# Deformable sampling by matrix multiplication: twelve column tiles of 11 in place of eleven of 12

## The chip, the cores and the metric

The kernel runs on one core of a Trainium2 chip. A core has TensorE (PE, the matrix engine; its weight loads are shown apart as PEld), VectorE (DVE), ScalarE (ACT), GpSimd (POOL) and SyncE (SP, which here only issues DMAs). The metric is the device time of one execution in microseconds (us); three runs of the kernel before give a median of 6642.1 us. "ns of one" is the mean duration of one instruction in one profiled execution.

## The reference

The input is x, 2 images of 256 channels and 128 x 128 pixels, float32. Two layers follow each other. In the first, a group-normalised x goes through three branches that differ in their dilation (1, 9, 12). Each branch predicts an offset for each of 9 taps and each pixel, samples the image bilinearly at the moved place, weights the nine samples per channel and adds them; a layer norm and a GELU follow. Their sum, a 1x1 convolution and a small MLP with two layer norms end the layer. The second layer is a 3x3 convolution with weights quantised to three values. Cut to the part that the change touches:

```python
off = _conv(x, w_off, pad, dil)                      # 18 planes: dy, dx of 9 taps
py = yy[None, None] - pad + ky * dil + off[:, :, 0]  # ky, kx: the tap
px = xx[None, None] - pad + kx * dil + off[:, :, 1]
sampled = _bilinear(x, py, px)                       # [B, C, 9, H, W]
y = jnp.einsum('bckhw,ck->bchw', sampled, w.reshape(C, 9))
```

## The kernel before

**Stages.** Stage A (to about 920 us) normalises x, writes it with the pixels as rows into a table in DRAM (`tables`, a row of 256 channels for every pixel of a padded image WT columns wide), predicts the offsets and writes "hats": for each tap, pixel and row or column of a window, the bilinear weight. Stage B (920 to 5700 us) samples and runs the MLP. Stage C (from 5700 us) is the second layer's convolution.

**Sampling.** A bilinear sample is a weighted sum over pixels near the unmoved place, so a tile of output columns is one matrix product. A window is RI = 2 rows of the padded image, which gives 66 windows per image, 132 in all. The 132 padded columns (W + 2 * REACH) are cut into NT = 11 tiles of CI = 12. A tile's sources are TR x TC = 6 x 16 = 96 pixels, two more on each side, so PX = 96 partitions. `load_tiles` (L1316) loads them from the table, 96 KB per tile, into buffers named xs; there are 18. For each window and branch (a "unit", 396 of them) `build` (L1353) multiplies row hats hy and column hats hx on DVE into A, 96 partitions x 9 taps x 2 rows x 156 columns (L1367). `sample` (L1442) then runs two passes, one per half of the channels. In a pass each tile is one product (L1468): the pixels of the tile are the stationary operand, the A of that tile's columns for all 9 taps and 2 rows are the moving one, 18 runs of 12 columns, 216 in all. In the profile a float32 product is two MATMUL instructions, each with its LDWEIGHTS. The result lands in PSUM, in one of four banks `pm` that hold two tiles each; ScalarE copies a bank to `ev` (L1480, or L1488 where taps are missing). A pass has six banks: tile 0 alone, then (1,2), (3,4) to (9,10). Then `accumulate` (L1375) adds the nine taps into a ring of image rows: one activation per new row on ScalarE (L1411), the others on VectorE (L1429). There are three `ev` buffers, two A, three hy and three hx.

`columns` (L1431) names which of the three column taps reach a tile at all. With dilation 12 the first and the last tile lack one column tap, so their product is 144 columns instead of 216. The columns of a tile which lie in the padding are computed all the same and not used.

**Order.** TensorE, VectorE and ScalarE run stage B in program order (`pin`). The MLP, layer norms and the rest of the first layer are written as generators, and `tail.advance()` runs a piece of them once at the beginning of a pass and once in its middle (L1458), so their matmuls (L890, L905, L1133, L1137, L1154) stand between the banks of the sampling. All loads of stage B are issued by SP, in an order that a scheduler lays down: per window 11 loads of xs and 18 of hats. A load of xs waits until the product that last read its buffer is done. With 18 buffers and 11 tiles in use, 7 tiles of the next window are loaded early, and its last four follow when tiles 0 to 3 of the present window have been read for the last time, in its sixth pass.

**Constants that hang on CI.** WT is the width of the table; XCLS lists the tap shifts modulo CI, for the patterns with which stage A forms the column hats; SPAN is how far from a tile's middle an offset may reach before a separate list of missed samples is used.

Of the kernel before, what the change touches and what calls it, by code (L numbers as in the profile page):

```python
# [9 lines left out]
F32 = mybir.dt.float32  # L10
# [10 lines left out]
W = 128  # L21
C = 256
# [6 lines left out]
DILS = (1, 9, 12)  # L29
# [8 lines left out]


REACH = 2  # L40
RI, CI = 2, 12
TR, TC = RI + 2 * REACH, CI + 2 * REACH
NT = -(-(W + 2 * REACH) // CI)
PX = TR * TC
WT = NT * CI + 2 * REACH
AO = 12
WA = 28 + W
NH = TR + TC + 2
# [5 lines left out]
PEAK = 4  # L54
GAP = 2
LAG = 7
XCLS = (0, 1, 3, 9, 11)
SLOTS = 42
ROWS = P
EACH = 2  # L60
SPAN = (REACH + (RI - 1) / 2, REACH + (CI - 1) / 2)
NPAT = RI + len(XCLS) + 1


# [7 lines left out]
def conv_preact_kernel(ctx: ExitStack, tc: tile.TileContext, t: dict, out: bass.AP):  # L72
    nc = tc.nc
    x = t["x"]
    NB, _, H, _ = x.shape
# [84 lines left out]

    tables = scratch.tile([NB * HT * WT, C], F32, name="tables")
    table = [tables[b * HT * WT : (b + 1) * HT * WT] for b in range(NB)]

# [46 lines left out]
    reach = const.tile([P, 2, NB * H], F32, name="reach")  # L210
# [110 lines left out]
    def phase_a(b, pool, psum, k, beside, todo):  # L321
        mean, rstd = gn1[b]
        tv = table[b].rearrange("(y x) c -> y x c", x=WT)
        zero = k["zero"]

        for y0, y1 in ((0, 2 * REACH), (2 * REACH + H, HT)):
            for yy in range(y0, y1):
                for x0 in range(0, WT, P):
                    n = min(P, WT - x0)
                    nc.sync.dma_start(tv[yy, x0 : x0 + n, :], zero[0:n])  # L330
        for x0, x1 in ((0, 2 * REACH), (2 * REACH + W, WT)):
            for xx in range(x0, x1):
# [170 lines left out]
    def missing(psum, pool, tabs):  # L503

        def tmp(name, rows, n, dt=F32):
            return pool.tile([rows, n], dt, name=name, tag=name, bufs=1)
# [11 lines left out]
        top = tmp("top", P, 8)  # L518
        nc.vector.tensor_scalar(V, reach[:, 0], SPAN[0], None, ALU.is_gt)
        nc.vector.scalar_tensor_tensor(V, reach[:, 1], SPAN[1], V, ALU.is_gt, ALU.max)  # L520
        nc.vector.tensor_reduce(cnt, V, AX.X, ALU.add)
# [84 lines left out]
        for d in range(2):  # L606
# [3 lines left out]
            for c in range(2):  # L610
                nc.vector.tensor_scalar(cd[:, c], cd[:, c], SPAN[c] ** 2, None, ALU.is_le)
            cov.append(cd)
# [95 lines left out]
    with ExitStack() as actx:  # L708
# [24 lines left out]
        for b in range(NB):  # L733
            stats = ap.tile([P, KC, NGRP, 6], F32, name=f"stats1_{b}", tag=f"stats1_{b}")
            for c in range(KC):
                for g0 in range(0, NGRP, XT):
                    xt = ap.tile([P, XT * NG], F32, name="xt", tag="xt", bufs=3)
# [527 lines left out]
    def sample_near(pool, psum, k):  # L1265

        pin = tc.keep_in_program_order
# [8 lines left out]
        xts, hbs, owners, begun = {}, {}, {}, set()  # L1276
# [38 lines left out]

        def load_tiles(b, Rt):  # L1316

            xts[b, Rt] = []
            for T in range(NT):
                xt = pool.tile([PX, C], F32, name="xs", tag="xs", bufs=18)  # L1320
                src = bass.AP(
                    table[b].tensor,
                    table[b].offset + (Rt * RI * WT + T * CI) * C,
                    [[C, TC], [WT * C, TR], [1, C]],
                )
                nc.sync.dma_start(xt, src)
                xts[b, Rt].append(xt)

        def taps(u):
            return [ky for ky in (-1, 0, 1) if valid(units[u][1], units[u][2], ky)]  # L1330
# [99 lines left out]

        def columns(br, T):  # L1431

            dil = DILS[br]
            kept = [
                i
                for i, s in enumerate((-dil, 0, dil))
                if max(0, REACH + s) < (T + 1) * CI
                and T * CI < min(W + 2 * REACH, W + REACH + s)
            ]
            return kept[0] * RI, (kept[-1] + 1) * RI  # L1440

        def sample(u, c):  # L1442

            b, Rt, br = units[u]
            kys = taps(u)
            tail.advance()
            if not kys:
                tail.advance()
                if c == KC - 1:
                    prepare(u + 2)  # L1450
                return
            A = k["A"][u % len(k["A"])].rearrange("p (y t) i w -> p y (t i) w", y=3)
            y0, y1 = kys[0] + 1, kys[-1] + 2
            n = (y1 - y0) * 3 * RI * CI
            ev = pool.tile([P, 9 * RI, NT * CI], F32, name="ev", tag="ev", bufs=3)
            evv = ev.rearrange("p (y m) w -> p y m w", y=3)
            for T in range(-1, NT, 2):
                if T == 2 * ((NT + 1) // 4) - 1:  # L1458
                    tail.advance()
                ts = range(max(T, 0), T + 2)  # L1460
                pm = k["pm"][tail.banks % len(k["pm"])]
                tail.banks += 1
                pv = pm[:, :, 0:n].rearrange("p j (y m w) -> p j y m w", y=y1 - y0, w=CI)
                reach = [columns(br, t) for t in ts]
                for j, t in enumerate(ts):
                    m0, m1 = reach[j]
                    pin(
                        nc.tensor.matmul(  # L1468
                            pv[:, j, :, m0:m1, :],
                            lhsT=xts[b, Rt][t][:, c * P : (c + 1) * P],  # L1470
                            rhs=A[:, y0:y1, m0:m1, AO + t * CI : AO + (t + 1) * CI],
                            start=True,
                            stop=True,
                        )
                    )
                m0, m1 = min(r[0] for r in reach), max(r[1] for r in reach)
                if m1 - m0 == 3 * RI:
                    dst = ev[:, y0 * 3 * RI : y1 * 3 * RI, ts[0] * CI : (ts[-1] + 1) * CI]
                    pin(
                        nc.scalar.copy(  # L1480
                            dst.rearrange("p m (t j) -> p t m j", j=CI),
                            pm[:, 0 : len(ts), 0:n].rearrange("p t (m j) -> p t m j", j=CI),
                        )
                    )
                else:
                    assert len(ts) == 1
                    pin(
                        nc.scalar.copy(  # L1488
                            evv[:, y0:y1, m0:m1, ts[0] * CI : (ts[0] + 1) * CI],
                            pv[:, 0, :, m0:m1, :],  # L1490
                        )
                    )
            if c == KC - 1:
                prepare(u + 2)
            accumulate(u, c, ev, kys)

        def prepare(u):

            if u < len(units):
                for ky in taps(u):  # L1500
                    build(u, ky)
                    load_hats(items.index((u, ky)) + 3)

        items = [(u, ky) for u in range(len(units)) for ky in taps(u)]
        load_hats(0)
        load_tiles(*units[0][0:2])
        load_hats(1)
        load_hats(2)
# [5 lines left out]
        for u, (b, Rt, br) in enumerate(units):  # L1514
            if u % len(BRS) == 0 and u + len(BRS) < len(units):
                load_tiles(*units[u + len(BRS)][0:2])
            for c in range(KC):
                sample(u, c)
            if u == 1:
                tail.extra = lacking(pool, tail.tile, miss, pin)  # L1520

            for b, br, g in begins[u]:
                r0 = g * R % RINGS[br]
                ring = k["rings"][br][:, :, r0 : r0 + R, :].rearrange("p k r w -> p k (r w)")
                tail.begin(tail.branch(b, br, g, ring), LAG)
                if br == 0:
                    begun_groups += 1
                    spot(begun_groups)
# [93 lines left out]
    with tc.If(beyond > 0) as cmp:  # L1622
        with ExitStack() as bctx:
            psum = bctx.enter_context(tc.tile_pool(name="ps_g", bufs=1, space=PSUM))
            pool = bctx.enter_context(tc.tile_pool(name="gpool", bufs=1))
            for b in range(NB):
                sample_any(b, pool, psum)
    with cmp.Else():
        with ExitStack() as bctx:
            psum = bctx.enter_context(tc.tile_pool(name="ps_b", bufs=1, space=PSUM))  # L1630
            pool = bctx.enter_context(tc.tile_pool(name="bpool", bufs=1))
# [359 lines left out]
```

## Time and profile before

| | |
|---|---|
| median of 3 runs | 6642.1 us (6639.65 to 6650.33) |
| profiled execution, its own time | 6632.7 us |
| its span on the core | 6630.8 us |
| stage B in it | 920 to 5700 us, 4780 us |
| mean granted TensorE clock | 0.974 |
| VectorE busy, share of the span | 89% |
| ScalarE busy, share of the span | 63% |
| loads of xs, whole run | 1452 of 96 KB |
| loads of hy and of hx, whole run | 1112 and 1112 in the page's row, of 288 KB |

A group's row names the line, the engine, the operation, what it writes and reads, the shape and the count; then the busy time and the mean duration of one; then the idle time of the engine just before such instructions and what ended it. A MATMUL's duration includes its latency: two that follow each other overlap in the record, and what one costs is the distance from its start to the next one's start. The chain of waits goes back from the last instruction through what released each, and gives each line's share of the time.

### The profile page before, as it was taken

How to read it: one execution, taken by the hardware profiler on the slowest of the kernel's cores; microseconds unless marked ns; L12 is line 12 of the kernel's file. 1: busy time of each engine (PE TensorE's matmuls, PEld its weight loads, DVE VectorE, ACT ScalarE, POOL GpSimd, SP SyncE). 2: the span in 40 equal slices, each digit the busy share in tenths (PEclk: the TensorE clock that was granted, in tenths of full speed). 3: DMA queues.
4: the chain of work that ended last, by engine and by line, in shares of the span. 5: the costliest groups of instructions: out<-in, count | busy, mean ns of one | idle time of the engine just before them, and what ended most of it. 6: DMA issues, size and time to landing. Idle time of an engine off the chain costs nothing.

```text
span 6630.8 us, 100591 instructions
## 1 busy us (share of the span) xinstructions
PE 6275.4 (95%) x32242; PEld 4993.0 (75%) x32242; DVE 5906.2 (89%) x13772; ACT 4189.3 (63%) x8690; POOL 686.7 (10%) x665
## 2 busy tenths in 40 slices
PE   6899978999999999999999999999999999989999
PEld 3455558888888888888888888888888888734444
DVE  8766668999999999999778999999999999689996
ACT  2344447777777777777676777777777777554442
POOL 0000000111111111111110111111111111200000
PEclk9999978999999999999999999999999999989999
DMA  8976667877787777787667877788777777343332
GB/s 290 274 214 199 201 169 216 226 217 219 223 225 217 223 217 224 222 222 206 181 194 203 227 219 219 221 223 227 223 217 220 215 222 209 122 164 132 139 139 90
DMA packets 635795, 1360.49 MB, mean 205 GB/s; under 512 B 109592, under 2 KB 290344, under 8 KB 618736
## 3 DMA queue, kind: packets, MB, share of 16 engines
q1 hardware_dynamic: 617328, 1318.97, 68.9%
q10 hardware_dynamic: 17408, 33.56, 1.6%
q8 instruction: 261, 4.28, 0.3%
q14 instruction: 286, 2.34, 0.1%
q0 software_dynamic: 512, 1.34, 0.1%
HBM read 1087.10 MB, written 266.47 MB: 204 GB/s over the span
## 4 chain that ended last, share of the span: by engine, by line
PE 53%; DVE 30%; DMA 8%; ACT 5%; issue 3%; SPq 0%; POOL 0%; DVEq 0%; ACTq 0%; POOLq 0%
PE pm L1468 22%; DVE ring L1429 13%; PE pc L1810 6%; PE hp L890 6%; PE h L1137 5%; DVE A L1367 5%; PE pz L364 4%; DMA hx<-hats 3%; PE pc L1137 3%; DMA xa<-in_x 3%; ACT ev L1480 2%; ACT v L1115 2%; DVE st L1101 1%; PE ph L463 1%; PE tp L905 1%
## 5 line engine op out<-in xcount | busy, mean ns | idle before, releaser
L1468 PE MATMUL pm<-A,xs 96*128 96x216 f32 (+2 forms) x17424 | 3248.5, 343 | 176.4 <-ACT ev L1480 45.4
L1468 PEld LDWEIGHTS pm<-A,xs 96*128 96x128 f32 x17424 | 3049.1, 195 | 374.1 <-ACT ev L1480 119.2
L1429 DVE SCALAR_TENSOR_TENSOR ring<-ev,defw,ring 128x256 f32<-128x256 f32 (+4 forms) x6372 | 2481.2, 451 | 98.1 <-ACT ev L1480 47.8
L1480 ACT COPY ev<-pm 128x432 f32<-128x432 f32 (+4 forms) x4488 | 1987.5, 483 | 869.3 <-PE pm L1468 695.8
L1367 DVE TENSOR_TENSOR A<-hy,hx 96x768 f32<-96x768 f32 (+1 forms) x1124 | 1009.5, 945 | 164.1 <-DMA hx<-hats 89.8
L1107 POOL TENSOR_TENSOR rs<-rs,mhalf 128x4 f32<-128x4 f32 x320 | 472.0, 1475 | 4202.5 <-DVE rs L1106 3543.9
L1810 PE MATMUL pc<-cring,signs 128*128 128x512 bf16 x3456 | 757.9, 382 | 17.0 <-ACT cring L1727 7.4
L1115 ACT ACTIVATE v<-v,rs 128x256 f32<-128x256 f32 x1280 | 694.4, 594 | 16.7 <-POOL rs L1108 16.6
L1810 PEld LDWEIGHTS <-signs 128*128 128x128 bf16 x3456 | 339.6, 98 | 434.6 <-issue 27.7
L890 PE MATMUL hp<-S,w 128*128 128x512 f32 x1024 | 493.9, 607 | 0.8 <-ACT S L1221 0.8
L364 PE MATMUL pz<-wz,xa 128*128 128x486 f32 x1024 | 461.6, 578 | 25.3 <-DVE zr L371 25.3
L1137 PE MATMUL h<-w,hT 128*128 128x256 f32 x2048 | 477.1, 379 | 0.0
L1101 DVE BATCH_NORM_STATS2 st<-v 128x6 f32<-128x256 f32 x1280 | 446.9, 410 | 30.8 <-ACT v L921 30.8
L1411 ACT ACTIVATE ring<-ev,defw 128x256 f32<-128x256 f32 (+1 forms) x856 | 404.5, 485 | 24.2
L1137 PEld LDWEIGHTS h<-w,hT 128*128 128x128 f32 x2048 | 369.3, 190 | 65.5 <-issue 1.0
L364 PEld LDWEIGHTS pz<-wz,xa 128*128 128x128 f32 x1024 | 189.2, 191 | 189.3 <-issue 126.1
L921 ACT COPY v<-tp 128x512 f32<-128x512 f32 x384 | 207.8, 598 | 182.7 <-PE tp L913 182.4
L1230 ACT ACTIVATE hT<-hp,b 128x512 f32<-128x512 f32 x256 | 176.1, 688 | 218.6 <-PE hp L890 214.6
L890 PEld LDWEIGHTS hp<-S,w 128*128 128x128 f32 x1024 | 196.7, 197 | 139.4 <-issue 121.3
L470 ACT ACTIVATE hb<-ph 96x512 f32<-96x512 f32 (+1 forms) x384 | 209.8, 596 | 144.2 <-PE ph L463 135.6
L1137 PE MATMUL pc<-convw,xn 128*128 128x256 f32 x1024 | 271.1, 393 | 2.4 <-ACT xn L1202 2.4
L371 ACT COPY zr<-pz 128x486 f32<-128x486 f32 x128 | 72.1, 564 | 256.5 <-PE pz L364 253.8
(246 smaller groups left out, 5132.5 us busy)
## 6 DMA issues: line engine op xcount, KB each, us to landing
hy<-hats SPq DMA_DIRECT2D x1112, 288.0 KB
hx<-hats SPq DMA_DIRECT2D x1112, 288.0 KB
xs<-tables SPq DMA_DIRECT2D x1452, 96.0 KB
g12d<-v SPq DMA_DIRECT2D x128, 512.0 KB
other<-g12d SPq DMA_DIRECT2D x128, 512.0 KB
hats<-hb SPq DMA_DIRECT2D x64, 720.0 KB
hats<-hb SPq DMA_DIRECT2D x64, 576.0 KB
xa<-in_x ACTq DMA_DIRECT2D x64, 512.0 KB
```

Source lines behind the costliest of these rows:

```text
L364: nc.tensor.matmul(pz[:, 0:NZ], lhsT=xt[:, c, r, :], rhs=k["wz"][:, c, :], start=c == 0, stop=c == KC - 1,)
L890: nc.tensor.matmul(out, lhsT=w, rhs=v, start=i == 0, stop=i == n - 1)
L1101: pin(nc.vector.bn_stats(st[:, j, :], rows[j]))
L1107: nc.gpsimd.tensor_tensor(rs[:, 0, :], rs[:, 0, :], mhalf[:, 0:n], ALU.pow)
L1115: nc.scalar.activation(row, row, func, scale=rs[:, 0, j : j + 1], bias=rs[:, 1, j : j + 1])
L1137: nc.tensor.matmul(bank[:, j, :], lhsT=v[:, px], rhs=w, start=False, stop=i == len(pairs) - 1,)
L1367: nc.vector.tensor_tensor(dst, hy[:, i0:i1].rearrange("p i t w -> p t i w"), hx[:, i0:i1].rearrange("p i t w -> p t i w"), ALU.mult,)
L1411: pin(nc.scalar.mul(dst, src, w))
L1429: pin(nc.vector.scalar_tensor_tensor(dst, src, w, dst, ALU.mult, ALU.add))
L1468: nc.tensor.matmul(pv[:, j, :, m0:m1, :], lhsT=xts[b, Rt][t][:, c * P : (c + 1) * P], rhs=A[:, y0:y1, m0:m1, AO + t * CI : AO + (t + 1) * CI],
L1480: nc.scalar.copy(dst.rearrange("p m (t j) -> p t m j", j=CI), pm[:, 0 : len(ts), 0:n].rearrange("p t (m j) -> p t m j", j=CI),)
L1810: nc.tensor.matmul(pc, lhsT=signs[:, k, (h * 3 + t) * 3 + kx, m * P : (m + 1) * P], rhs=xc[:, i, k, t * JC : (t + 1) * JC, kx : kx + W], s ...
```

## The change

The 132 padded columns are cut into 12 tiles of 11 columns. A tile's sources stay 6 x 16 pixels, so the loads still fill 96 partitions: 2 columns before the tile and 3 after it. WT goes from 136 to 137. The banks of a pass are (1,2), (3,4) to (9,10) and, last, the pair of the first and the last tile (0,11); these two are loaded last. `columns` now also gives the first and last column that any tap uses, and a product covers only those; its result lies densely in its half of the bank. All six copies take two tiles. The buffers xs go from 18 to 19. The piece of the tail in the middle of a pass comes after two banks (four tiles) in place of three banks (five tiles).

```diff
-RI, CI = 2, 12
-TR, TC = RI + 2 * REACH, CI + 2 * REACH
+RI, CI = 2, 11
+TR, TC = RI + 2 * REACH, 16
 NT = -(-(W + 2 * REACH) // CI)
-WT = NT * CI + 2 * REACH
+WT = (NT - 1) * CI + TC
+SIDE = (TC - 1) / 2
-XCLS = (0, 1, 3, 9, 11)
+XCLS = (0, 1, 2, 9, 10)
-SPAN = (REACH + (RI - 1) / 2, REACH + (CI - 1) / 2)
+SPAN = (REACH + (RI - 1) / 2, SIDE)
...
-            xts[b, Rt] = []
-            for T in range(NT):
-                xt = pool.tile([PX, C], F32, name="xs", tag="xs", bufs=18)
+            xts[b, Rt] = {}
+            for T in (*range(1, NT - 1), 0, NT - 1):
+                xt = pool.tile([PX, C], F32, name="xs", tag="xs", bufs=19)
...
-            dil = DILS[br]
-            kept = [
-                i
-                for i, s in enumerate((-dil, 0, dil))
-                if max(0, REACH + s) < (T + 1) * CI
-                and T * CI < min(W + 2 * REACH, W + REACH + s)
-            ]
-            return kept[0] * RI, (kept[-1] + 1) * RI
+            p0, p1 = T * CI, (T + 1) * CI
+            kept, lo, hi = [], p1, p0
+            for i, s in enumerate((-DILS[br], 0, DILS[br])):
+                a, z = max(p0, 0, REACH + s), min(p1, W + 2 * REACH, W + REACH + s)
+                if a < z:
+                    kept.append(i)
+                    lo, hi = min(lo, a), max(hi, z)
+            return kept[0] * RI, (kept[-1] + 1) * RI, lo, hi
...
-            for T in range(-1, NT, 2):
-                if T == 2 * ((NT + 1) // 4) - 1:
+            edges = (0, NT - 1)
+            for ts in [(t, t + 1) for t in range(1, NT - 1, 2)] + [edges]:
+                if ts[0] == NT // 2 - 1:
                     tail.advance()
...
-                    m0, m1 = reach[j]
+                    m0, m1, p0, p1 = reach[j]
+                    w, n = p1 - p0, (y1 - y0) * (m1 - m0) * (p1 - p0)
                     pin(
                         nc.tensor.matmul(
-                            pv[:, j, :, m0:m1, :],
+                            pm[:, j, 0:n].rearrange(
+                                "p (y m w) -> p y m w", y=y1 - y0, w=w
+                            ),
                             lhsT=xts[b, Rt][t][:, c * P : (c + 1) * P],
-                            rhs=A[:, y0:y1, m0:m1, AO + t * CI : AO + (t + 1) * CI],
+                            rhs=A[:, y0:y1, m0:m1, AO + p0 : AO + p1],
...
+                (ma, mb, pa, _), (md, _, pd, pe) = reach
+                first = evv[:, y0:y1, ma:mb, pa : pa + w]
+                step = (md - ma) * NT * CI + pd - pa
...
+                dst = bass.AP(
+                    first.tensor, first.offset, [dims[0], [step, 2]] + rows + [dims[3]]
+                )
...
+                pin(nc.scalar.copy(dst, src))
```

## The prediction

> **What bounds the kernel now.** I read the page's shares first, then the busy times of stage B alone, then the chain of waits of that stage, then the timeline of TensorE, for the price of one product. The page:
>
> ```profile
> span 6630.8 us, 100591 instructions
> PE 6275.4 (95%) x32242; PEld 4993.0 (75%) x32242; DVE 5906.2 (89%) x13772; ACT 4189.3 (63%) x8690; POOL 686.7 (10%) x665
> ```
>
> Stage B alone (columns: stretch, its length, then busy us and instructions of each engine, granted clock, DMA share, GB/s) and its chain of waits:
>
> ```profile
> 920.00:5700.00 4780.00, 4614.24 (x24864) 4115.21 (x24865) 4451.02 (x11227) 3415.48 (x7664) 653.15 (x618) 0.98 0.77 216
> ...
> by line: PE pm L1468 31.0%; DVE ring L1429 17.5%; PE hp L890 7.3%; PE h L1137 6.4%; DVE A L1367 6.3%; DMA hx<-hats 4.5%; PE pc L1137 3.4%; ACT ev L1480 3.3%; issue 3.2%; ACT v L1115 2.1%; DVE st L1101 1.9%; PE tp L905 1.8%; DMA xs<-tables 1
> ```
>
> TensorE is idle for 166 of 4780 us, VectorE for 329: both are nearly full, TensorE more so. The chain says the same: over half of it is TensorE, some 26% VectorE (ring, A, st). So a stretch of TensorE time saved is not a stretch of kernel time saved wherever VectorE leads.
>
> Now the price of a product, from TensorE's timeline (start, length of the merged group, what, count):
>
> ```profile
> 3028.74 2.35 PE L1468 MATMUL pm<-A,xs 96*128 96x216 f32 x12
> 3030.93 0.27 PE L1133 MATMUL h<-row,ones 128*128 128x256 bf16 x1
> 3031.05 1.89 PE L1137 MATMUL h<-w,hT 128*128 128x256 f32 x8
> 3032.77 0.27 PE L1133 MATMUL h<-row,ones 128*128 128x256 bf16 x1
> ```
>
> Twelve instructions of 216 columns take 3030.93 - 3028.74 = 2.19 us, 183 ns each; eight of 256 columns take 1.72 us, 215 ns each. Both are 0.845 ns per column: there is no fixed price per product at these sizes, although the first reads 18 runs of 12 columns and the second one run. In the records of the smaller forms of L1468 the starts are 123 ns apart for 144 columns (again 0.85 each) but 112 ns for 72: below about 131 columns a floor holds.
>
> The waits of the line, and the two kinds of copy (rows: group, count | busy, mean ns | idle before, releasers):
>
> ```profile
> L1468 PE MATMUL pm<-A,xs 96*128 96x216 f32 x14304 | 2846.4, 352 | 126.6 <-ACT S L1221 41.5 <-ACT ev L1480 27.8 <-ACT ev L1488 23.4
> L1480 ACT COPY ev<-pm 128x432 f32<-128x432 f32 x3440 | 1680.5, 524 | 523.1 <-PE pm L1468 490.3
> L1480 ACT COPY ev<-pm 128x216 f32<-128x216 f32 x480 | 156.2, 326 | 228.6 <-DVE ring L1429 122.7 <-PE pm L1468 101.9 <-PE tp L913 3.7
> L1488 ACT COPY ev<-pm 128x144 f32<-128x144 f32 x208 | 55.9, 269 | 87.5 <-DVE ring L1429 76.1 <-PE pm L1468 9.5 <-DVE st L1101 1.6
> ```
>
> ScalarE waits mostly for products; the first copy of a pass (216 or 144) waits for VectorE to free an `ev`. A copy costs about 0.9 ns per element: (524 - 326) / 216.
>
> **What the Trainium skill says.** "TensorE: Matmul & The Clock Gate", section Back-to-back issue gap, gives N / 2.4 + 2.5 ns for a warm stream, so a cost by columns; the trace agrees in kind, at two cycles per column for each of a float32 product's two instructions. The same page, section LDWEIGHTS, prices a weight load by its columns, P / 1.2, 107 ns for 128; the measured floor of 112 ns fits it. "Perfetto Trace Analysis", section Matmuls, says larger matmuls are more efficient; from 144 to 256 columns the trace shows no difference. "SBUF — State Buffer", section Door 1, says SBUF has 16-byte lines and that crossing into a new one costs; runs of 12 floats that begin on a line, as now, show no such price, and runs of 11 are not in this trace.
>
> **The change part by part.**
>
> *Products, removed and added.* With all three row taps, a pass costs before 11 x 216 = 2376 columns (dilations 1 and 9) or 9 x 216 + 2 x 144 = 2232 (12). After: ten tiles of 18 x 11 = 198, and two edge tiles: 18 x 10 = 180 each with dilation 1 (columns 1 to 10 and 121 to 130 of the padded image), 12 x 11 = 132 each with 9 and 12, as one column tap never reaches them. That is 2340, 2244 and 2244. So the cut into 11s as such costs nothing (12 x 198 = 11 x 216), and what is saved is the padding and, with dilation 9, a tap at each edge. Over all windows, those with fewer row taps included, the compiled instruction list of the kernel before has 7152 products of 216, 1200 of 144 and 360 smaller; that of the kernel after 6880 of 198, 512 of 180, 1664 of 132 and 448 of at most 88. At 0.845 ns per column, not less than 111, two instructions each: 2983 us before, 2929 after, so **-54 us of TensorE**. The 792 more products are in this, and their loads of weights lie behind the matmuls as now.
>
> *How much reaches the end.* The chain holds line 1468 for 0.31 x 4780 = 1482 us, half of its 2983; at that share -27 us. If TensorE led all through, -54. TensorE is the fuller engine and its idle time is only 3.5%, so I take somewhat over half: -34 us. What is late next is VectorE: ring and A.
>
> *Copies.* Six per pass as before, 1,706,336 elements per partition in place of 1,762,944: -56,600 x 0.9 ns = -51 us of ScalarE. The chain has 3.3% x 4780 = 158 us of some 2150 us of copies, 7%: -4 us. The pass's last copy, which `accumulate` waits for, goes from 524 to about 458 (360 elements) or 370 ns (264); VectorE waited for ev only 51 times, 47.8 us: -2 us. The first goes from 326 or 269 to about 491 ns, and when ScalarE has waited there for VectorE, TensorE gets its bank some 0.2 us later; some 110 such waits, in which VectorE leads and TensorE has all four banks full anyway: between 0 and +22, taken as +3. The last copy writes a four-step pattern (two tiles, rows, taps, columns); L1488 writes a three-step one at 269 ns for 144 elements, no dearer than L1480's 280. I add nothing; its upper end, 50 ns in 792 passes, is 40 us of ScalarE, which is idle 29% of the stage, so +3 at most.
>
> *Loads.* 132 more xs loads, 12.7 MB on the stage's 216 GB/s x 4780 us = 1032 MB, 1.2%. The chain waits for DMAs for about 6%, 290 us: +3 us if those stretch in step, 0 if they are latency. Each costs SP about 0.55 us of issue (x1452, median 546 ns), 73 us in all; SP often waits for the products that free a buffer, 780 us over the run, so it has the room. In the compiled order each window's xs still stand ahead of the next window's need. Buffer reuse: 19 against 12 in use leaves 7 early ones, as 18 against 11 did. The last five wait for tiles 1 to 5, read in banks 1 to 3 of the sixth pass, and are needed from bank 4 of the next: nine or ten banks between, as before. The last-loaded tile, 11, is behind hats in SP's queue in some windows, but these wait for builds that are earlier still. Products wait for xs only 27 us now, most at the stage's start.
>
> *Edits with one answer:* the tail's middle piece after four tiles in place of five moves nothing between engines; XCLS has five entries still; the window's reach stays 7.5; build, hats and accumulate keep their shapes. In stage A one more column of zeros per image is a 128-row DMA each, and the row fills are longer by one pixel: +1 us. Stage B's start has one more load ahead of its first last bank: +1.
>
> *Sum:* -34 - 4 - 2 + 3 + 3 + 1 + 1 = -32 us. The profiled execution took 6632.7 us, so 6601 in such a one; the median shown lies 9 us above it, so **6610 us** against 6642.
>
> **Rivals.**
>
> *TensorE leads throughout.* For it: 96.5% busy, and a shorter product frees banks earlier. Against it: VectorE is at 93%. All of -54 and -6 of copies, +5: 6587.
>
> *VectorE leads.* The stage cannot be shorter than 4451 us of VectorE plus its own waits; if the gap left is already what the hand-overs need, under a quarter of the saving arrives: -8, 6634. For it: from 4000 to 5000 us VectorE is busy 966 us of 1000, TensorE 976. Against it: in other stretches TensorE alone makes the chain for 50 us on end.
>
> *Short runs cost (slower).* Place: TensorE reading A. Today each run begins on a 16-byte boundary; runs of 11 do not. A price per unaligned run is seen in this trace: at L1810 (bf16, four runs of 128) products whose columns begin at an odd 2-byte place start 219 ns apart, the others 216, so 0.8 ns per run. If float32 runs paid that, 18 x 0.8 = 14 ns on 13,760 instructions and less on the small ones are +230 us of TensorE; if only runs off an 8-byte boundary, half of that. It decides from 54 us / 18,100 instructions = 3.0 ns per instruction, 0.17 per run. Half paid, net +61 of TensorE at 0.7: 6685. Against it: the L1810 runs that begin at 4, 8 or 12 bytes of a line pay nothing measurable, and every float32 begins at 4. The same doubt for ScalarE's writes of 11 is smaller, as ScalarE has room: 0 to +10.
>
> **How the numbers follow.** Forecast (6595 to 6625) 0.48; TensorE leads throughout 0.20; VectorE leads 0.15; short runs cost 0.17. A change under 0.2%, 13 us, cannot be told from none. Faster 0.68, same 0.15, slower 0.17. The range begins at 6575, below the full saving with some waits gone too, and ends at 6655, which takes in VectorE's case and a run price just past its break-even; it leaves out most of the slower one.
>
> **What would show it.** L1468 at 167 ns from start to start for 198 columns (more than 171 means that runs cost), 152 for 180, 112 for 132. Copies of 396 at about 491 ns. TensorE's busy time in stage B lower by some 50 us, VectorE's the same in a shorter stage, so nearer to full. No new waits for xs. I am wrong if the starts lie wider, if VectorE waits more for A's hats, or if the stage is as long as before with TensorE idler.

## The result and the profile after

The changed kernel takes 6705.4 us (median of 5 runs, 6700.1 to 6712.5) against 6640.7: a ratio of 1.0097, 95% interval 1.0082 to 1.0111. It is 65 us slower; the forecast was 6610. The profiled execution took 6703.4 us. First its span and shares, then stage B alone (columns: stretch, length, busy us and instructions of PE, PEld, DVE, ACT, POOL, granted clock, DMA share, GB/s), then the rows of the products and copies before and after, then the chain of waits of stage B:

```profile
span 6701.6 us, 103952 instructions
PE 6369.4 (95%) x33826; PEld 5129.5 (77%) x33826; DVE 5911.1 (88%) x13772; ACT 4242.7 (63%) x8690; POOL 671.0 (10%) x665
```

```profile
920.60:5772.50 4851.90, 4705.20 (x26455) 4252.46 (x26456) 4458.62 (x11238) 3469.27 (x7667) 638.84 (x620) 0.98 0.77 215
```

```profile
L1468 PE MATMUL pm<-A,xs 96*128 96x216 f32 (+2 forms) x17424 | 3248.5, 343 | 176.4 <-ACT ev L1480 45.4
...
L1480 ACT COPY ev<-pm 128x432 f32<-128x432 f32 (+4 forms) x4488 | 1987.5, 483 | 869.3 <-PE pm L1468 695.8
```

```profile
L1468 PE MATMUL pm<-A,xs 96*128 96x198 f32 (+3 forms) x19008 | 3329.3, 331 | 150.4 <-ACT ev L1495 52.8
...
L1495 ACT COPY ev<-pm 128x396 f32<-128x396 f32 (+2 forms) x4752 | 2074.3, 480 | 989.4 <-PE pm L1468 657.0
```

```profile
by line: PE pm L1468 35.9%; DVE ring L1430 10.4%; PE hp L891 8.8%; PE h L1138 8.4%; ACT ev L1495 5.3%; PE pc L1138 4.6%; ACT v L1116 3.5%; DMA hx<-hats 3.4%; DVE A L1368 3.4%; issue 2.8%; PE tp L906 2.4%; PE zc L1155 1.3%; PE tp L914 1.2%; 
```

Stages A and C keep their lengths (920 and 929 us). Stage B grows from 4780 to 4852 us, and TensorE's busy time in it by 91 us, from 4614 to 4705. The products' row goes from 3248.5 to 3329.3 us, though it now streams fewer columns. VectorE's busy time is the same (4451, 4459). In the chain, the products' share rises from 31.0 to 35.9% and VectorE's ring falls from 17.5 to 10.4%: TensorE has become dearer and leads more of the stage.

The price of one product shows where. TensorE's timeline of the changed kernel (start, length of the merged group, what, count):

```profile
3042.66 1.58 PE L1468 MATMUL pm<-A,xs 96*128 96x198 f32 x8
3044.07 1.88 PE L891 MATMUL hp<-S,w 128*128 128x512 f32 x4
3045.79 2.93 PE L1468 MATMUL pm<-A,xs 96*128 96x198 f32 x16
3048.56 1.88 PE L891 MATMUL hp<-S,w 128*128 128x512 f32 x4
```

Eight instructions of products from 3042.66 to 3044.07 are 176 ns each, sixteen from 3045.79 to 3048.56 are 173 ns, where 198 x 0.845 = 167 was forecast. This is a mean of two prices. The table gives the median distances from one MATMUL's start to the next one's, worked out from the two traces and sorted by the tile, and how the tile's runs lie on 16-byte lines (four floats). The floats of a line that a run uses are its hits in the texts below:

```
kernel, tiles                              run begins   floats per line  lines  ns
before, all (12 columns)                   0 of 4       4 4 4            3      182 to 186
after, tiles 4, 8 (11 columns)             0 of 4       4 4 3            3      167 to 168
after, tiles 3, 7                          1 of 4       3 4 4            3      167
after, tiles 2, 6, 10                      2 of 4       2 4 4 1          4      184 to 186
after, tiles 1, 5, 9                       3 of 4       1 4 4 2          4      187 to 189
after, tiles 0, 11, dilation 1 (10)        1, 1 of 4    3 4 3            3      152 to 153
```

Six of twelve tiles pay some 20 ns in each of their two instructions, about 1.1 ns per run. It isn't alignment as such: runs that begin one float into a line are free, and runs that begin two floats into it (8-byte aligned) pay. What the paying ones have in common is a fourth line, and a line of which they use a single float; the experiments tell these two apart. With 688 passes that have all row taps, 6 x 688 x 2 x 20 ns is 165 us.

ScalarE's copies split in the same way, as they write the same runs of 11 into `ev`. Where the engine had been idle before it, a copy of tiles (3,4) or (7,8) takes 489 to 490 ns, one of (1,2), (5,6) or (9,10) takes 532 to 534, and before, with runs of 12 on the line, 518.

### The profile page after: what moved, and what is told of

Read it like the earlier page. It is cut to its first block, busy times and chain, and to the rows that moved or that the text cites. A ratio compares the mean times of both kernels' runs of the same rounds, so it can differ in the third digit from the quotient of the medians.

```text
span 6701.6 us, 103952 instructions
## 1 busy us (share of the span) xinstructions
PE 6369.4 (95%) x33826; PEld 5129.5 (77%) x33826; DVE 5911.1 (88%) x13772; ACT 4242.7 (63%) x8690; POOL 671.0 (10%) x665
## 4 chain that ended last, share of the span: by engine, by line
PE 60%; DVE 21%; ACT 8%; DMA 7%; issue 3%; SPq 0%; POOL 0%; DVEq 0%; ACTq 0%; POOLq 0%
PE pm L1468 26%; DVE ring L1430 8%; PE hp L891 7%; PE h L1138 7%; PE pc L1813 6%; PE pz L365 4%; ACT ev L1495 4%; PE pc L1138 4%; ACT v L1116 3%; DMA xa<-in_x 3%; DMA hx<-hats 2%; DVE A L1368 2%; PE tp L906 2%; PE ph L464 1%; PE zc L1155 1%
## 5 line engine op out<-in xcount | busy, mean ns | idle before, releaser
L1468 PE MATMUL pm<-A,xs 96*128 96x198 f32 (+3 forms) x19008 | 3329.3, 331 | 150.4 <-ACT ev L1495 52.8
L1468 PEld LDWEIGHTS pm<-A,xs 96*128 96x128 f32 x19008 | 3201.4, 193 | 305.8 <-ACT ev L1495 110.3
L1495 ACT COPY ev<-pm 128x396 f32<-128x396 f32 (+2 forms) x4752 | 2074.3, 480 | 989.4 <-PE pm L1468 657.0
L1108 POOL TENSOR_TENSOR rs<-rs,mhalf 128x4 f32<-128x4 f32 x320 | 456.8, 1427 | 4289.0 <-DVE rs L1107 3464.3
```

Of the source, the lines that this page charges most:

```text
L1108: nc.gpsimd.tensor_tensor(rs[:, 0, :], rs[:, 0, :], mhalf[:, 0:n], ALU.pow)
L1468: nc.tensor.matmul(pm[:, j, 0:n].rearrange("p (y m w) -> p y m w", y=y1 - y0, w=w), lhsT=xts[b, Rt][t][:, c * P : (c + 1) * P], rhs=A[:, y ...
L1495: pin(nc.scalar.copy(dst, src))
```

## The experiments

**Does the price move with the address?** A shifted by one float in the changed kernel.

```diff
-AO = 12
+AO = 13
```

> The changed kernel with every column of A one float further on (AO = 13 in place of 12); nothing else moves. In the changed kernel's trace the products of tiles 3, 4, 7, 8 start 167 ns apart, those of 1, 2, 5, 6, 9, 10 start 184 to 189 ns apart. Theory 1 (a run pays about 1 ns when one of the 16-byte lines that it touches is hit by a single float): the price moves with the runs, tiles 2, 3, 6, 7, 10 at 184 to 189 ns, tiles 1, 4, 5, 8, 9 at 167, and tile 11 of the dilations 9 and 12 at 123 to 126 in place of 112; ScalarE's copies, whose target does not move, keep 490 and 532 ns; time a little less, 6680 to 6705. Rival (the place of the tile in the pass, its bank or its load makes it slow): the same six tiles stay slow, time 6705.

Measured: 6693.9 us, ratio 1.0082 (1.0065 to 1.0099). The price moved as theory 1 had it: tiles 2, 3, 6, 7, 10 at 184 to 188 ns, tiles 1, 4, 5, 8, 9 at 167 to 171, tile 11 of dilations 9 and 12 at 123 to 124 in place of 112 to 113; the copies kept 489 and 533. Place in the pass, bank and load are out as causes; the address decides.

**What in the address?** Two shifts of the kernel before, whose runs have 12 columns: by two floats, as the diff shows, and by one (AO = 13).

```diff
-AO = 12
+AO = 14
```

> The kernel before with A two floats further on (AO = 14): its runs of 12 then touch four 16-byte lines with 2, 4, 4, 2 hits. Theory 1 (single hits pay): L1468 stays at 183 ns from start to start, time 6641 within 15. Theory 2 (each line beyond three pays, or any start off a 16-byte line): 183 + 18 x 1.03 = 202 ns, TensorE has some 290 us more, time 6830 to 6950.

> The kernel before with A one float further on (AO = 13): every run of 12 hits lines 3, 4, 4, 1 times, so each has a single hit and touches four lines. Theories 1 and 2 both: L1468 at about 202 ns for 216 columns, some 290 us more of TensorE; as TensorE then leads everywhere, time 6850 to 6940. If the price came only with runs of odd length (11), or from the changed order: 183 ns and 6641.

Measured: shift by two 6654.1 us, ratio 1.0022 (1.0013 to 1.0030), starts mostly 185 to 187 ns apart; shift by one 6701.9 us, ratio 1.0101 (1.0085 to 1.0118), starts mostly 191 to 194. A group of the second in the timeline:

```profile
3038.59 2.48 PE L1468 MATMUL pm<-A,xs 96*128 96x216 f32 x12
```

(2.48 - 0.36) / 11 is 193 ns. Both theories missed: theory 2's 202 ns did not come, though all these runs touch four lines, and theory 1's full price for a single hit (3, 4, 4, 1) did not come either: 8 to 10 ns in place of 19. But 12 columns in four lines (186) and 11 columns in four lines (186) cost the same. So I formed theory G: a run costs as much as its columns, or as three columns for each line that it touches, whichever is more. Four lines then cost 12 columns: +1 column for a run of 11 (18 x 0.845 = 15 ns), nothing for one of 12 apart from a remainder of 3 to 10 ns.

**The changed kernel with cuts at even columns.** Tiles of 10 and 12 columns, so that no line is hit once.

```diff
-RI, CI = 2, 11
+RI, CUT = 2, (0, 10, 22, 34, 46, 58, 70, 82, 92, 102, 112, 122, 132)
...
-            p0, p1 = T * CI, (T + 1) * CI
+            p0, p1 = CUT[T], CUT[T + 1]
...
-        pattern[RI + i] = ((np.arange(W) + REACH + m) % CI)[None, :]
+        pattern[RI + i] = phase(np.arange(W) + REACH + m)[None, :]
...
```

> The changed kernel with its order, pairs, loads and 12 tiles, but the cuts between tiles at even columns: widths 10, then six of 12, four of 10, and 10. No run then has a line with a single hit, in A or in ev. Columns per pass 2340, 2256, 2256, near the 2340, 2244, 2244 of the changed kernel. Theory 1: 183 ns for 216 columns, 152 for 180, copies at 518 and 0.8 ns per element less; TensorE some 50 us below the kernel before, time 6595 to 6625. Theory 2: the tiles of 12 that begin two floats into a line pay, 202 ns, time 6700 to 6800. Rival (the order, the edge pair at the end or the 132 more loads cost the time): no better than the changed kernel, 6690 to 6720.

Measured: 6683.2 us, ratio 1.0072 (1.0055 to 1.0088): a miss. The prices of products are near what theory 1 and G have (186 ns for 216 columns, 152 for 180), but TensorE's busy time does not fall, 6294 us against 6275: the six tiles of 12 begin two floats into a line and pay the remainder of 3 ns, and products of 120 columns (edges of dilations 9 and 12) often stand at the floor of 112 ns, so fewer columns are not less time. Stage A is 15 us longer in this kernel (its first product starts at 935 us), which has two more patterns. With the 12 us that the further loads cost in a run below, 15 or so of the 42 us are left; they are not taken apart further.

**Theory G against single hits**, on the same kernel.

```diff
-AO = 12
+AO = 13
```

> The kernel with even cuts and A one float further on. It tells apart what is paid for. Theory G (a run costs as much as its columns or as three columns for each 16-byte line that it touches, whichever is more): tiles 7 to 10 (10 columns, hits 1, 4, 4, 1 or 3, 4, 3): those that begin three floats into a line touch four lines and take the time of 12 columns, 183 to 190 ns in place of 152; tile 11 of dilation 1 (9 columns, hits 1, 4, 4, three lines) stays at 138. Theory S (a line hit once costs a stall of some 1 ns per run): tile 11 of dilation 1 goes to 150 to 156 ns, and the 10-column tiles with two single hits to about 188. A look, not a time.

Measured (one execution, of which only the distances are used): tiles 7 and 9 (10 columns, hits 1, 4, 4, 1) at 182 for the first and 186 to 187 ns for the second instruction of a product, in place of 152; tiles 8 and 10 (3, 4, 3) at 152 to 156; tile 11 of dilation 1 (9 columns, hits 1, 4, 4) at 140 in place of 138. The last decides: a line hit once costs next to nothing when the run touches three lines. Theory S falls; theory G fits all these prices within some 12 ns. By it the price applies to short runs: lines of which fewer than three floats are used on average.

The traces say one thing more. Their clock records show stretches in which TensorE runs at half clock, 336 us in all in the changed kernel. There 198 columns take 329 ns with three lines and 332 with four (medians of 78 and 99 distances), and in the kernel of this run 180 columns take 299 and 300. At half clock the fourth line is all but free. So a line takes a time rather than a number of columns: by estimate about 2.6 ns, from 186 ns for 18 runs of four lines. That is three columns at full clock, and at half clock it hides behind the columns.

**Order and loads alone**, on the kernel before.

```diff
-            for T in range(NT):
+            for T in (*range(1, NT), 0):
...
-            for T in range(-1, NT, 2):
-                if T == 2 * ((NT + 1) // 4) - 1:
-                    tail.advance()
-                ts = range(max(T, 0), T + 2)
+            for ts in [(t, t + 1) for t in range(1, NT, 2)] + [(0,)]:
+                if ts[0] == 5:
+                    tail.advance()
```

> The kernel before, its 11 tiles of 12 and 18 buffers kept, but in the order of the changed one: banks (1,2) to (9,10) first and the single tile 0 last, loaded last, and the tail's middle piece after two banks. Price of a run and number of loads are as before. Theory O (beside the price of the runs, the new order of the banks costs stage B some 15 to 35 us, because a pass then begins with a copy of two tiles, 518 ns, after VectorE has freed an ev): 6655 to 6675. Theory P (the price of the runs is all): 6641 within 13.

Measured: 6641.5 us, ratio 1.0000 (0.9989 to 1.0012). The order costs nothing that can be told from the noise (8 us); theory O falls.

```diff
-            for T in range(NT):
-                xt = pool.tile([PX, C], F32, name="xs", tag="xs", bufs=18)
+            for T in (*range(NT), 0):
+                xt = pool.tile([PX, C], F32, name="xs", tag="xs", bufs=19)
```

> The kernel before with a twelfth load of xs per window, a second copy of tile 0 that no product reads, and 19 buffers: the loads and buffers of the changed kernel with the products of the one before. Theory L (the 132 more loads, on SP's queue and the DMA engines, cost 15 to 35 us): 6655 to 6675. Theories O and P: 6641 within 13.

Measured: 6653.3 us, ratio 1.0018 (1.0008 to 1.0028). The loads cost about 12 us (5 to 19). That is more than the forecast's 4, less than theory L named and within the 13 us that theories O and P left open.

**The edge pair first**, in the changed kernel.

```diff
-            for T in (*range(1, NT - 1), 0, NT - 1):
+            for T in (0, NT - 1, *range(1, NT - 1)):
...
-            for ts in [(t, t + 1) for t in range(1, NT - 1, 2)] + [edges]:
+            for ts in [edges] + [(t, t + 1) for t in range(1, NT - 1, 2)]:
```

> The changed kernel with the edge pair (0,11) as the first bank of a pass and loaded first; the tail's middle piece then comes after three banks. The runs' price stays (same products). Theory O: 15 to 30 us come back, 6675 to 6690. Theories P and L: 6705 within 10.

Measured: 6697.0 us, ratio 1.0074 (1.0060 to 1.0087), beside the changed kernel's 1.0097 (1.0082 to 1.0111). The intervals overlap: some 8 us, if anything, and less than theory O asked for.

**The price taken out of the changed kernel.**

```diff
-                            rhs=A[:, y0:y1, m0:m1, AO + p0 : AO + p1],
+                            rhs=A[:, y0:y1, m0:m1, AO + p0 // 4 * 4 : AO + p0 // 4 * 4 + w],
```

> The changed kernel where every product reads its columns of A from the 16-byte line in which they begin, so that each run touches three lines. This computes another thing: up to three columns of weights to the left of the right ones are used, so its output is not the reference's. Instructions, shapes, order, loads and copies are those of the changed kernel. If the price of the runs in TensorE's reads is what made the change slower: L1468 at 167 ns throughout, TensorE some 150 us less than in the changed kernel, time 6625 to 6655, that is, about the kernel before. If the rest of the change (loads, copies of 11, order) costs more than its share: 6670 to 6700.

Measured: 6646.4 us, ratio 1.0010 (1.0000 to 1.0021), 59 us under the changed kernel. The row of the products and a group in the timeline:

```profile
L1468 PE MATMUL pm<-A,xs 96*128 96x198 f32 (+3 forms) x19008 | 3211.4, 326 | 197.6 <-ACT ev L1495 101.6
```

```profile
3014.10 2.79 PE L1468 MATMUL pm<-A,xs 96*128 96x198 f32 x16
```

(2.79 - 0.31) / 15 = 165 ns, about the forecast's 167. The row is 118 us shorter than in the changed kernel and 37 us shorter than in the kernel before. So the price of the fourth line is some 59 of the 65 us (12 us either way by the two intervals). The run also shows a second fault of the forecast: with that price gone and TensorE's saving there, the kernel takes 6 us more than the one before (0 to 14), where 32 less were forecast.

**ScalarE's price alone**, on the kernel before.

```diff
-            ev = pool.tile([P, 9 * RI, NT * CI], F32, name="ev", tag="ev", bufs=3)
+            ev = pool.tile([P, 9 * RI, NT * CI + 4], F32, name="ev", tag="ev", bufs=3)[:, :, 1 : NT * CI + 1]
```

> The kernel before with ev four floats wider and its columns one float further on: ScalarE's copies then write runs of 12 with 3, 4, 4, 1 hits. TensorE's reads stay as they are. In the changed kernel a copy of two paying tiles took 533 ns against 490. If ScalarE's writes have a price of their own: copies of 432 at 530 to 560 ns in place of 518, and a time within 13 us of 6641, as ScalarE is idle 29% of stage B. If ScalarE's time counts as much as TensorE's: 6660 to 6690.

Measured: 6649.7 us, ratio 1.0013 (1.0004 to 1.0021).

```profile
L1480 ACT COPY ev<-pm 128x432 f32<-128x432 f32 x3440 | 1770.1, 555 | 463.1 <-PE pm L1468 442.1
```

The copies went from 524 to 555 ns, in all 90 us of ScalarE on this row, and the time by 9 us. So ScalarE's writes have a price too, and it counts about a tenth. Here runs of 12 in four lines do pay (33 ns for 36 runs, 551 against 518 after idle time), so theory G is shown for TensorE's reads alone.

**What a saving of TensorE is worth here.**

```diff
-                            pv[:, j, :, m0:m1, :],
+                            pv[:, j, :, m0:m1, 0 : CI - 1],
...
-                            rhs=A[:, y0:y1, m0:m1, AO + t * CI : AO + (t + 1) * CI],
+                            rhs=A[:, y0:y1, m0:m1, AO + t * CI : AO + (t + 1) * CI - 1],
```

> The kernel before where every product leaves out the last of its 12 columns (the runs keep their places, hits 4, 4, 3, three lines); those columns of ev then hold older values, so a twelfth of the samples is not computed. Nothing else changes. It asks what TensorE time saved alone is worth here: 18 columns x 0.845 = 15 ns of each of some 14,300 instructions of 216 and less on the others, about 240 us of TensorE less. The forecast took somewhat over half of a saving to reach the end: -120 us or more, 6520 or below. If VectorE takes over at once, as the run with aligned reads suggests (TensorE's work 22 us under the kernel before, no time gained): less than a third, 6560 to 6630.

Measured: 6599.2 us, ratio 0.9931 (0.9914 to 0.9947). Its page, the shares and the chain by engine:

```profile
PE 6155.6 (93%) x32242; PEld 4853.4 (73%) x32242; DVE 5901.9 (89%) x13772; ACT 4177.5 (63%) x8690; POOL 686.7 (10%) x665
...
DVE 41%; PE 40%; DMA 10%; ACT 5%; issue 4%; SPq 1%; DVEq 0%; POOL 0%; ACTq 0%; POOLq 0%
```

The same line of the kernel before, and stage B of this run (columns as above):

```profile
PE 53%; DVE 30%; DMA 8%; ACT 5%; issue 3%; SPq 0%; POOL 0%; DVEq 0%; ACTq 0%; POOLq 0%
```

```profile
920.00:5675.00 4755.00, 4490.82 (x24854) 3973.83 (x24855) 4448.41 (x11229) 3401.53 (x7662) 655.98 (x620) 0.96 0.78 217
```

Some 240 us of TensorE by columns gave 41 us, a sixth. By the page's busy time only 120 us were saved, and 41 is a third of that. VectorE's part of the chain went from 30 to 41%, TensorE's from 53 to 40%: VectorE takes over. Part of what is missing between 240 and 120 is the granted clock, which stands at 0.959 to 0.962 in this kernel's six runs and at 0.970 to 0.976 in the eleven of the kernel before. This trace has 532 us at half clock, where 198 columns take 331 ns in place of 167; the trace before has 341. By estimate the 191 us more are worth up to 95 us of TensorE, half of them. The run with aligned reads shows it too, with 411 us at half clock. How much of a saving goes to the clock and how much to VectorE is not separated, and why the clock was granted less is not tested.

In the other direction, by the page's busy time, shift by one adds 111 us of TensorE and 61 to the time, the changed kernel 94 and 65, shift by two 36 and 13: between a third and two thirds. By this measure time added and time saved do not differ much.

**A version that may beat both**, by little: the kernel before, with the one unused column of dilation 1 left out at each edge, where the runs of 11 touch three lines.

```diff
-            return kept[0] * RI, (kept[-1] + 1) * RI
+            lo, hi = (1 if dil == 1 and T == 0 else 0), (CI - 1 if dil == 1 and T == NT - 1 else CI)
+            return kept[0] * RI, (kept[-1] + 1) * RI, lo, hi
...
-                            pv[:, j, :, m0:m1, :],
+                            pv[:, j, :, m0:m1, lo:hi],
...
-                            rhs=A[:, y0:y1, m0:m1, AO + t * CI : AO + (t + 1) * CI],
+                            rhs=A[:, y0:y1, m0:m1, AO + t * CI + lo : AO + t * CI + hi],
```

> The kernel before, where the products of the first and the last tile of dilation 1 leave out the one column that no tap uses (columns 0 and 131): runs of 11 that begin one float into a line (3, 4, 4 hits) or on one (4, 4, 3), which touch three lines and should cost 167 ns in place of 183. Four instructions per window, half and pass pair less by 16 ns each, some 17 us of TensorE less over the run; 6630 to 6641. If every run of 11 paid, no gain.

Measured: 6636.7 us, ratio 0.9990 (0.9980 to 0.9999), some 6 us, at the edge of what can be told from none. The trimmed products start 167 to 171 ns apart: runs of 11 in three lines are cheap in this kernel too.

## Why the prediction was wrong

*Products.* This is the step that failed: "there is no fixed price per product at these sizes", and from it "At 0.845 ns per column, not less than 111, two instructions each: 2983 us before, 2929 after". The column counts were right, and so was the price for every tile whose runs touch three lines (167, 152 and 112 ns, as listed under what would show it). It did not hold for the six tiles with four lines, 184 to 189 ns. Every run of A that these products read in the kernel before was 12 floats on a line, so its trace could not show the difference. Of the 97 us between the forecast's -32 and the measured +65, this step has some 59. (The floor is looser than "below about 131 columns a floor holds": in the trace before, the first instruction of a 96-column product in the last tile takes 83 ns.)

*The rival that came true.* "Short runs cost" named the place and the sign, and half of its price gave 6685. It had the mechanism in part only, as it let every run off a line pay, or every run off an 8-byte boundary; those that begin one float into a line are free, and those that begin two floats into it pay. I held it at 0.17 because of "the L1810 runs that begin at 4, 8 or 12 bytes of a line pay nothing measurable". Those runs are 128 bf16 long, 16 or 17 lines each, so nearly all their lines are full; a run of 11 floats has three or four. The evidence was about another shape. The Trainium skill's page "SBUF — State Buffer", section Door 1, which says that crossing into a new 16-byte line costs, was the better guide, and I set it aside because aligned runs showed no price. The trace agrees that lines matter, but not with the page's "need ≥2 hits per line": 9 columns with hits 1, 4, 4 took 140 ns in place of 138.

*How much reaches the end.* "I take somewhat over half: -34 us" failed as well. 240 us of TensorE by columns, saved alone, gave 41 us, and with aligned reads the changed kernel gained nothing. For savings the rival "VectorE leads" was the better reading of a VectorE that is 93% busy, though it too left out that the clock might be granted less. The chain's share of a line tells what it holds now; what a saving is worth depends on how soon the next engine takes over. VectorE had 329 us of idle time in stage B, and where TensorE was 240 us cheaper it still had 307 (4755 less 4448).

*Copies.* -51 us of ScalarE did not come: the row of 1987.5 and the 264 copies of L1488 (some 70 us) became the row of 2074.3. Copies of 396 elements were forecast at 491 ns; those of three-line tiles took 490, the others 533.

*Loads.* +4 was forecast, about +12 (5 to 19) measured on the kernel before; an upper end of 3 us for them was too small. What they displace is not shown.

*Right:* no new waits for xs (19.9 us in stage B against 23.2), stages A and C unchanged, VectorE's busy time unchanged, no price of the order and of the place of the tail's piece that stands out of the noise.

The sum is then the price of the fourth line, 59 us, and 6 more. These 6 fit loads of 12 and copies of up to 9, less what the 37 us of TensorE bring that the trimming saves, but the terms are as small as their intervals, so this split is not shown.

*Open:* why a line takes its 2.6 ns; the remainder of 3 to 10 ns at 12 columns in four lines; how a saving of TensorE divides between VectorE and the clock; and some 15 of the 42 us of the kernel of even cuts.

## What to carry to other kernels

Before a tile's width is changed, count how many 16-byte lines each innermost run of an operand touches, for every tile and not only the first: with short float32 runs a fourth line made 11 columns as dear as 12, and runs of 12 that begin on a line never touch a fourth. A price per column taken from a trace in which all runs are aligned says nothing about others; shifting the buffer by one float, an edit of one line, measures it. And where two engines are both over 90% busy, do not count a saving by its columns: of 240 us saved on one of them here, a sixth reached the end. Look at the granted clock of such a run as well as at the other engine.

## What the runs showed of the hardware

TensorE's float32 reads fit the larger of the run's columns and three columns per 16-byte line: 9 columns in three lines 138 to 140 ns (18 runs), 10 in three 152 to 156, 11 in three 167 to 171, 12 in three 182 to 186; 10, 11 and 12 columns in four lines 182 to 187, 184 to 189 and 185 to 195. At half clock the fourth line costs nearly nothing: 198 columns 329 and 332 ns, 180 columns 299 and 300. ScalarE's writes to SBUF of the same runs also pay, about 1.2 ns per run of 11 with a fourth line (533 against 490 ns for 36 runs) and 0.9 per run of 12 begun one float into a line (551 against 518). 132 additional loads of 96 KB, on DMA engines that are busy 77% of stage B, cost 12 us (5 to 19), though the products waited no longer for their tiles (18.8 us in stage B against 23.2). And the two kernels with cheaper products and a TensorE that idles more (11 of 12 columns, aligned reads) were granted a lower mean clock, 0.959 to 0.962 and 0.967 to 0.972, against 0.970 to 0.977.
